# K and V of the context for the second block: tiles of their own, and another place in the order of work

## The chip, the cores and the metric

The kernel runs on one core of one Trainium2 chip. The metric is the device time of one execution in microseconds (us). The core's engines work side by side, each on its own stream of instructions: TensorE (PE; its weight loads are listed apart as PEld), VectorE (DVE), ScalarE (ACT), GpSimd (POOL) and SyncE (SP), which here mostly issues DMAs. An engine works through its own instructions in their order, and waits on semaphores for what others make.

## What is computed

Two attention blocks follow each other, all in fp32. The tokens x are 2 x 1024 rows of 256 elements, the context ctx is 2 x 64 rows of 256, and there are 16 heads of 16. Cut to what matters:

```
# block 0
q  = ln(x);  x = x + mha(q, q)                      # self attention, 1024 keys
x  = x + mha(ln(x), ln(ctx))                        # cross attention, 64 keys
h  = ln(x)                                          # 8 experts, the best 2 for each token
vals, idx = top_k(h @ router, 2);  gates = softmax(vals)
x  = x + sum_k gates_k * expert_idx_k(h)            # 256 -> 1024, gelu, -> 256

# block 1
x  = x + self_attention(ln(x))
q  = heads(ln(x) @ q_w.T)
k  = heads(ctx @ k_w.T)                             # ctx as it comes in, no norm
v  = heads(ctx @ v_w.T)
x  = x + softmax(q k^T * scale + bias) v @ ca_proj_w.T
x  = x + fc2(gelu(fc1(ln(x))))
```

The k and v of block 1 depend on nothing but ctx and two weights. They could be made at any time before block 1's first cross attention.

## The kernel before

*Stages.* The self attention of a block is a sequence of 128 cells. A cell makes scores on PE (line 796), their maxima on DVE (803), scores less the maxima on PE (807), exponentials on ACT (813) and the product with V on PE (858). Other work, cut into generators that yield estimated costs, runs between the cells. A `Stream` holds these generators as tasks; a task may begin at a cell (`first`), must be done by a cell (`last`), has marks that it waits for (`after`) and a `rank`. Behind the last cell, `stream.rest` takes the ready task of the highest rank, one step at a time, and counts time by the costs that the steps yield; a step that yields zero or less makes its task not ready for a while. All this happens while the program is built. The result is a fixed order of instructions on PE, DVE, ACT and SP; POOL's order is set by the tile framework.

*Behind the first block's cells* (from about 596 us in the profiled execution) `stream.rest` has these left: the fourth cross attention (tokens 512 to 1023 of the second sequence), which consists of two halves; `dispatch_task` for units 2 and 3 of 512 tokens (the router's logits, line 1320; ranking within the experts, lines 1373 to 1409; writing of the sorted rows, scatters on POOL); `mixture.find` and `mixture.rows`; and the first five slots. A slot is 256 rows for one expert, its weights being loaded by DMA: transposes of its rows (1610), a first layer (1644), GELU on ACT (1650), a second layer (1674), and a scatter of its result to DRAM by POOL (1689). The ranks are: cross attention up to 67, finding 65, dispatch 70, rows 75, and slot s 10-s. `norm_task` and `turned` (360) norm and transpose tokens, `project_task` (428 and 436) is an output projection and its addition to x.

*Then* `mixture.run(5, 15)` emits slots 5 to 14, in the profile from about 730 to 935 us, and block 1's cells follow, with the remaining slots at their beginning.

*The context.* `context_load` issues the DMAs for a block's two context weights (512 KB, tile `w_ctx`) and for ctx, twice 64 KB (both halves of the partitions hold a copy). `context_task` makes, in this order: for block 0 a norm; four transposes of ctx (360, called by `turned`); for block 1 a copy of them (`kvT`, 1017); K's products (1025); four evictions to `kbd` (1037), in which every second head is zeroed by a column of scales; V's products (1047); eight copies to `vbd` (1058), which fill only every second group of 16 columns, the others having been set to zero by a memset in `other_constants`. `weigh`, the weighing of a cross attention, reads `kbd` in its score products (1131) and `vbd` in its products with V (1180).

`kbd` and `vbd` are one tile each, in the pool of the constants (lines 295 and 296), 4 KB of each partition together, and serve both blocks. The second block's context is written to them only after the first block's last cross attention has read them. Its task is advanced by hand within slots 5 to 14:

```
1965        for n, _ in enumerate(mixture.run(NFULL[-1], NFIRST)):
1966            if n > 16 and n % 2 == 0:
1967                next(context, None)
```

*Memory.* Pools are opened and closed in the program. `cpool0` and `dpool0` hold the tiles of block 0's cross attentions and dispatch and are closed by `tail.close()` (line 1956). `hpool`, opened after them in the room they leave, holds block 1's head tiles, `QS` and `KS` among them; `make_heads` fills their constant rows with copies and memsets on POOL. The right side holds the slots' pools (`slotw`, `epool`).

Of the kernel before, what the change touches and what calls it, by code (L numbers as in the profile page):

```python
# [41 lines left out]
F32 = mybir.dt.float32  # L42
# [8 lines left out]
P = 128  # L51
B, S, D, H, DH = 2, 1024, 256, 16, 16
# [149 lines left out]
def two_blocks(  # L202
# [89 lines left out]

    desc = const.tile([P, E], F32, name="desc")
    bias_out = [const.tile([P, D], F32, name=f"bias_out{i}") for i in range(2)]
    kbd = const.tile([P, 2, B, 2, SK], F32, name="kbd")
    vbd = const.tile([P, B, H // 2, 32], F32, name="vbd")

    def other_constants():
        nc.gpsimd.memset(restart, 1.0)
        nc.gpsimd.memset(restart[:, :, 0:1], 0.0)  # L300
        nc.gpsimd.memset(vbd, 0.0)

    maxima = [True]

# [685 lines left out]
    def context_load(layer, pool):  # L990

        w = pool.tile([P, NCTX], F32, tag="cq", name=f"w_ctx{layer}")
        nc.sync.dma_start(out=w, in_=ctx_w[layer])
        c = pool.tile([P, B, D], F32, tag="cx", name=f"ctx{layer}")
        for u in range(2):
            nc.sync.dma_start(
                out=c[SK * u : SK * (u + 1)], in_=ctx_in.rearrange("b k d -> k b d")
            )
        return w, c

    def context_task(layer, w, c, pool):

        att = 2 * layer + 1
        kv = pool.tile([P, 2, B * P], F32, tag="p1", name=f"kvT{layer}", bufs=4)

        def src(t):
            return c[:, t, :]

        if layer == 0:
            held = yield from statistics(src, B, "kv")  # L1010
            xns = center(src, range(B), held, "kv")
            yield 0.0
            i, tp = turned(xns)
            affine(kv, i, tp, "ckv")
        else:
            i, tp = turned([src(t) for t in range(B)])
            nc.scalar.copy(kv, tp)
            free.append(i)
        yield 1.0
        yield 0.0  # L1020
        i, pk = bank()
        pk = pk[:, : 2 * B * SK].rearrange("p (g b k) -> p g b k", g=2, b=B)
        for g in range(2):
            for k in range(2):
                nc.tensor.matmul(
                    pk[:, g],
                    lhsT=w[:, X_K + k * D + g * P : X_K + k * D + (g + 1) * P],
                    rhs=kv[:, k, :].rearrange("p (b c) -> p b c", b=B)[:, :, :SK],
                    start=(k == 0),
                    stop=(k == 1),  # L1030
                )
        yield 1.0

        for u in range(2):
            for g in range(2):
                bias = C_K[att] + 2 * u + g
                nc.scalar.activation(
                    kbd[:, g, :, u, :], pk[:, g], AF.Identity, bias=cols[:, bias : bias + 1],
                    scale=cols[:, C_U + u : C_U + u + 1],
                )  # L1040
            yield 0.3
        free.append(i)
        i, pv = bank()
        pv = pv.rearrange("p (b d) -> p b d", b=B)
        for b in range(B):
            for k in range(2):
                nc.tensor.matmul(
                    pv[:, b, :],
                    lhsT=kv[:, k, b * P : (b + 1) * P],
                    rhs=w[:, X_V + k * D : X_V + (k + 1) * D],  # L1050
                    start=(k == 0),
                    stop=(k == 1),
                )
        yield 2.0
        for u in range(2):
            half = slice(SK * u, SK * (u + 1))
            for b in range(B):
                nc.scalar.copy(
                    vbd[half, b, :, DH * u : DH * (u + 1)],
                    pv[half, b, :].rearrange("p (r v d) -> p r v d", v=2, d=DH)[:, :, u, :],  # L1060
                )
        free.append(i)
        yield 0.5
# [28 lines left out]
    def weigh(layer, b, pool, w, name, held):  # L1092

        att = 2 * layer + 1
        yield -1.4
        xT = held["xT"]
        q = pool.tile([P, 2, 512], F32, tag="cq", name=f"q_{name}")
# [741 lines left out]
    def block(layer, tail, heads=None, beside=None):  # L1839

        pools = {}

        def open_pools():
            side = {"side": "right"} if layer else {}
            for p in ("cpool", "dpool"):
                pools[p] = tail.enter_context(tc.tile_pool(name=f"{p}{layer}", bufs=1, **side))

        if layer == 0:
            open_pools()
        made, ys, ready = [], [], {}  # L1850

        def arrive(n):
            if layer == 1:
                engines = (nc.gpsimd if n else nc.vector, nc.vector)
                add_results(ys[n // 2][:, n % 2], n, engines)

        def extra(stream, vpool, at_cell):
            if layer == 0:
                t = vpool.tile([P, 8, WIDE], F32, tag="v", name="fill")
                nfill = NROWS // 512  # L1860
                for n in range(nfill):
                    at_cell(n + 2, lambda n=n: fill(t, n))
                at_cell(nfill + 2, lambda: stream.made.add("filled"))
                stream.add(
                    context_task(layer, *context_load(layer, pools["cpool"]), pools["cpool"]), 9.0,
                    last=30, mark="context",
                )
            else:
                at_cell(104, lambda: made.extend(forward_weights(vpool)))
                stream.made.add("context")  # L1870
                ys.extend(
                    vpool.tile([P, 2, 2, 2, D], F32, tag="v", name=f"y{i}") for i in range(3)
                )
                for n in range(4):
                    load_results(ys[n // 2][:, n % 2], n)

                def second_batch(n0):
                    for n in range(n0, n0 + 2):
                        load_results(ys[2][:, n % 2], n)
                    for n in range(n0, n0 + 2):  # L1880
                        add_results(ys[2][:, n % 2], n, (nc.gpsimd, nc.gpsimd))
                    if n0 == 6:
                        stream.made.add("arrived")

                at_cell(0, lambda: second_batch(4))
                at_cell(3, lambda: second_batch(6))

        def when_ready(b, qh, stream, cell):
            n = 2 * b + qh
            cross_tasks(stream, layer, n, pools["cpool"], cell + 1)  # L1890
            if layer == 0:
                stream.add(
                    dispatch_task(n, pools["dpool"], lambda: stream.made.add(("counted", n))), 7.0,
                    mark=("dispatch", n),
                    after=[("cross", n), "filled"] + ([("dispatch", n - 1)] if n else [])
                    + ([("found", n)] if n > 1 else []),
                    rank=70,
                )
                if n == 1:
                    stream.add(  # L1900
                        mixture.find(2), 0.3, mark=("found", 2), after=[("counted", 1)], rank=65
                    )
                    stream.add(
                        mixture.rows(2), 0.0, mark=("rows", 2), rank=75,
                        after=[("found", 2), ("dispatch", 1)],
                    )
            elif n < 2:
                stream.add(
                    forward_norm(n, pools["dpool"], made, ready), 3.0, first=106, mark=("ready", n),
                    after=[("cross", n)],  # L1910
                )

        def around(begin):
            beside(begin)
            open_pools()

        stream, later = self_attention(layer, tail, heads, arrive, extra, when_ready, around)
        return stream, later, made, ready
# [11 lines left out]
    slotw, epool = [], []  # L1930
    mixture = Mixture(slotw, epool)
    stream, later, _, _ = block(0, tail)
    slotw.append(slots.enter_context(tc.tile_pool(name="slotw", bufs=2, side="right")))
    for n in range(2):
        epool.append(
# [13 lines left out]
    for s in range(NFULL[-1]):  # L1949
# [2 lines left out]
            mixture.slot(s), 14.4, mark=("slot", s), rank=10 - s,  # L1952
            after=[("rows", units)] + ([("slot", s - 2)] if s > 1 else []),
        )
    stream.rest(later, 64 * B + 2)
    tail.close()
    hpool = ctx.enter_context(tc.tile_pool(name="hpool", bufs=1))
    load_attention(2)
    load_attention(3)
    heads = make_heads(hpool, 1)  # L1960
    with ExitStack() as passing:

        xpool = passing.enter_context(tc.tile_pool(name="xpool", bufs=1))
        context = context_task(1, *context_load(1, xpool), xpool)
        for n, _ in enumerate(mixture.run(NFULL[-1], NFIRST)):
            if n > 16 and n % 2 == 0:
                next(context, None)
        for _ in context:
            pass

    def beside(begin):

# [164 lines left out]
```

## The time and the profile before

| what | us |
|---|---|
| median of 3 runs | 1632.26 (1632.18 to 1632.59) |
| the profiled execution | 1638.78 |
| its span, from the first to the last instruction | 1637.0 |
| PE busy in the span | 1591.4 |
| from the last cell to the slots run by themselves, 596 to 730 | 134, PE busy 121.9 |
| slots 5 to 14, 730 to 935 | 205, PE busy 205.0 |

The profile is of one execution, which took 6.5 us more than the median of the runs without a profile. Its page in forty slices, from which the stages can be read:

```profile
PE   7999999999999998999999999999999999999998
...
DVE  5796767687678647421113457876867867855400
...
PEclk9898999999999998999999999999999999999999
DMA  5234311101000105276567321000110002000000
```

Each digit is the busy share of 41 us, in tenths. Slices 1 to 14 hold block 0's cells; then come the stretch behind them, with DMA rising and DVE falling, and the slots, where DVE is nearly idle; from slice 23 on, block 1. PEclk is the clock that PE was granted, in tenths of its full speed: it is 8 in the second and fourth slice, and again in the slice from 614 to 655 us, where the fourth cross attention stands.

In views of single instructions, `banks<-kvT,w_ctx 128*128 128x128` is a tile written, the tiles read and the shapes; `x8` counts records; what stands in square brackets is how long the engine waited before it and for what.

### The profile page before, as it was taken

To read this page: it belongs to the slowest core of one execution; us is meant where nothing else is said; L and a number is where in the kernel's file an instruction comes from. 1 tells how busy PE (TensorE), PEld (TensorE's weight loads), DVE (VectorE), ACT (ScalarE), POOL (GpSimd) and SP (SyncE) were. 2 spreads that over 40 slices of the span, in tenths; PEclk is the share of its full clock that TensorE was granted. 3 is DMA by queue.
4 is the path that set the end of the run, shared out by engine and by line. 5 is a ranking of instruction groups with operands and counts; after the bars stand their busy time and mean duration, and the time that the engine had idled before them with its cause. 6 is when DMAs were issued, how large, how long until landed. Compare 5 with 4: busy or idle time off the path is not lost.

```text
span 1637.0 us, 28319 instructions
## 1 busy us (share of the span) xinstructions
PE 1591.4 (97%) x10710; PEld 882.4 (54%) x10710; DVE 982.7 (60%) x2094; ACT 912.9 (56%) x1767; POOL 410.6 (25%) x545
## 2 busy tenths in 40 slices
PE   7999999999999998999999999999999999999998
PEld 3433444544543446878888753344344435446766
DVE  5796767687678647421113457876867867855400
ACT  3486767676765753333322327876776676674321
POOL 2243423134235202141112032411321323321010
PEclk9898999999999998999999999999999999999999
DMA  5234311101000105276567321000110002000000
GB/s 157 111 132 171 131 27 34 28 21 47 14 21 34 53 30 188 78 270 216 176 204 241 91 65 33 21 27 17 38 39 19 25 14 83 15 14 21 14 13 26
DMA packets 55751, 121.07 MB, mean 74 GB/s; under 512 B 12218, under 2 KB 26428, under 8 KB 55228
## 3 DMA queue, kind: packets, MB, share of 16 engines
q1 hardware_dynamic: 51772, 109.07, 20.9%
q0 software_dynamic: 3456, 9.51, 1.6%
q8 instruction: 86, 1.41, 0.4%
q10 hardware_dynamic: 384, 0.66, 0.2%
q14 instruction: 53, 0.43, 0.1%
HBM read 71.68 MB, written 38.88 MB: 68 GB/s over the span
## 4 chain that ended last, share of the span: by engine, by line
PE 89%; DVE 7%; issue 1%; ACT 1%; DMA 1%; another core or an unknown queue 1%; POOL 0%; SPq 0%; DVEq 0%; POOLq 0%; ACTq 0%
PE banks L807 16%; PE banks L796 15%; PE banks L858 14%; PE banks L1674 8%; PE banks L1644 8%; PE banks L626 4%; PE banks L428 3%; PE banks L1816 3%; PE banks L1804 3%; DVE mx_s L803 3%; PE banks L1131 2%; PE banks L596 2%; PE banks L1167 2%; PE banks L360 2%; PE banks L1101 2%
## 5 line engine op out<-in xcount | busy, mean ns | idle before, releaser
L803 DVE TENSOR_REDUCE mx_s<-banks 128x1 f32<-128x512 f32 x1024 | 634.7, 682 | 221.2 <-PE banks L796 214.9
L813 ACT ACTIVATE pt_s<-banks 128x512 f32<-128x512 f32 x1024 | 532.6, 609 | 155.5 <-PE banks L796 124.4
L796 PE MATMUL banks<-KS,QS 16*128 16x512 f32 x2048 | 539.5, 633 | 4.0 <-ACT part_s L870 1.6
L807 PE MATMUL banks<-qb_s,KS 32*128 32x512 f32 x2048 | 519.2, 623 | 6.6 <-DVE qb_s L706 3.7
L871 POOL TENSOR_TENSOR acc_s<-acc_s,part_s 128x512 f32<-128x512 f32 x141 | 179.4, 1272 | 442.2 <-ACT part_s L870 441.5
L807 PEld LDWEIGHTS banks<-qb_s,KS 32*128 32x128 f32 x2048 | 181.3, 187 | 178.6 <-DVE mx_s L803 104.4
L858 PE MATMUL banks<-pt_s,v_s 128*20 128x512 f32 x2048 | 264.1, 607 | 1.5 <-DVE mx_s L803 1.0
L796 PEld LDWEIGHTS banks<-KS,QS 16*128 16x128 f32 x2048 | 201.1, 186 | 76.8 <-issue 37.3
L1674 PE MATMUL banks<-w_slot,h_s 128*128 128x256 f32 x640 | 145.4, 383 | 3.0 <-ACT h_s L1650 3.0
L858 PEld LDWEIGHTS banks<-pt_s,v_s 128*20 128x20 f32 x2048 | 43.2, 99 | 187.5 <-ACT pt_s L813 132.1
L1674 PEld LDWEIGHTS banks<-w_slot,h_s 128*128 128x128 f32 x640 | 121.7, 192 | 23.5 <-ACT h_s L1650 3.4
L870 ACT COPY part_s<-banks 128x512 f32<-128x512 f32 x155 | 92.7, 598 | 65.1 <-PE banks L858 54.5
L1683 DVE SCALAR_TENSOR_TENSOR ys<-banks,gate,b 128x256 f32<-128x256 f32 x40 | 19.3, 483 | 174.2 <-PE banks L1674 166.3
L1650 ACT ACTIVATE h_s<-banks,w_slot 128x256 f32<-128x256 f32 x104 | 43.7, 471 | 111.6 <-issue 65.3
L1689 POOL DMA_INDIRECT results<-ys,to x40 | 38.7, 967 | 255.0 <-DVE ys L1683 211.2
L1644 PE MATMUL banks<-xsT,w_slot 128*128 128x256 f32 x416 | 95.6, 381 | 0.7 <-ACT xsT L367 0.7
L1644 PEld LDWEIGHTS banks<-xsT,w_slot 128*128 128x128 f32 x416 | 77.4, 190 | 14.9 <-DVE mx_s L803 2.3
L1152 POOL TENSOR_TENSOR sc_c<-sc_c,mx_c 128x512 f32<-128x512 f32 x38 | 40.0, 1054 | 102.4 <-DVE mx_c L1151 102.4
L626 PE MATMUL banks<-xT_s,w_att 128*128 128x512 f32 x128 | 64.7, 642 | 0.0
L1807 ACT ACTIVATE h_f<-banks,w_ff 128x512 f32<-128x512 f32 x32 | 22.0, 687 | 73.9 <-PE banks L1804 73.9
L1650 ACT ACTIVATE h_s<-banks,spare 128x256 f32<-128x256 f32 x56 | 23.4, 471 | 62.8 <-issue 31.3
L1816 PE MATMUL banks<-w_ff,h_f 128*128 128x256 f32 x256 | 57.3, 380 | 0.0
(269 smaller groups left out, 1651.4 us busy)
## 6 DMA issues: line engine op xcount, KB each, us to landing
w_slot<-in_ff_w_dram SPq DMA_DIRECT2D x40, 576.0 KB
sorted_rows<-fill SPq DMA_DIRECT2D x36, 520.0 KB
w_slot<-in_ff_w_dram SPq DMA_DIRECT2D x26, 514.0 KB
whole<-acc_s SPq DMA_DIRECT2D x30, 256.0 KB
spare<-in_ff_w_dram SPq DMA_DIRECT2D x14, 514.0 KB
xs<-sorted_rows SPq DMA_DIRECT2D x20, 260.0 KB
y<-results SPq DMA_DIRECT2D x16, 256.0 KB
QS<-stq_s SPq DMA_DIRECT2D x124, 32.0 KB
```

The costliest lines, as they stand in the source:

```text
L626: nc.tensor.matmul(p, lhsT=w[:, at + k * D + pair * P : at + k * D + (pair + 1) * P], rhs=xT[b][:, k, blk * 512 : (blk + 1) * 512], start= ...
L796: nc.tensor.matmul(sc, lhsT=QS[h % 4][r, qc * P : (qc + 1) * P], rhs=K[r, kh * 512 : (kh + 1) * 512], start=True, stop=True,)
L803: return i, lambda: nc.vector.tensor_reduce(mx[h][:, qc, j, kh : kh + 1], sc, AX.X, ALU.max)
L807: nc.tensor.matmul(sc, lhsT=K[r, n * P : (n + 1) * P], rhs=QB[h][r, :], start=True, stop=True)
L813: nc.scalar.activation(pt, sc, AF.Exp, scale=SCALE)
L858: nc.tensor.matmul(o[32 * j : 32 * j + VW, :], lhsT=V[b][:, cell % 8, 4 * g + j, :], rhs=exps.pop((cell, j)), start=(cell == cells[0]), st ...
L870: nc.scalar.copy(part, o)
L871: helper().tensor_tensor(acc[h], acc[h], part, ALU.add)
L1644: nc.tensor.matmul(ph[:, n, :], lhsT=w[:, at : at + P], rhs=xT[:, k, :], start=(k == 0), stop=(k == 1),)
L1650: nc.scalar.activation(h1[:, f, :], ph[:, n, :], AF.Gelu, bias=w[:, W_B1 + f : W_B1 + f + 1])
L1674: nc.tensor.matmul(py, lhsT=h1[:, f, h * P : (h + 1) * P], rhs=w[:, f * D : (f + 1) * D], start=(f == 0), stop=(f == 7),)
L1816: nc.tensor.matmul(py[:, n, :], lhsT=h1[:, f, t * P : (t + 1) * P], rhs=w2[:, f * D : (f + 1) * D], start=(f == 0), stop=(f == 7),)
```

## The change

`kbd` and `vbd` become two pairs, one for each block, made by a new function `context_places`. The first block's pair stands in its `cpool0`; the second's in a new pool `kpool` on the right side, opened behind the first block's cells, with a memset of its `vbd` on POOL there. `context_task` and `weigh` pick the pair of their block.

With that the second block's context no longer has to follow the first block's last reads. Its task is now a task of the stream behind the first block's cells, of rank -20 (every other task there stands above it) and cost 6.0; `context_load` is called where the task is added, so its three DMAs are issued there. Its tiles stand in `xpool`, which is now open around `stream.rest`. `mixture.run(5, 15)` runs with nothing between.

```diff
@@ two_blocks
-    kbd = const.tile([P, 2, B, 2, SK], F32, name="kbd")
-    vbd = const.tile([P, B, H // 2, 32], F32, name="vbd")
+    kbds, vbds = {}, {}
+
+    def context_places(layer, pool):
+
+        kbds[layer] = pool.tile([P, 2, B, 2, SK], F32, name=f"kbd{layer}")
+        vbds[layer] = pool.tile([P, B, H // 2, 32], F32, name=f"vbd{layer}")
+
 
     def other_constants():
...
-        nc.gpsimd.memset(vbd, 0.0)
+        nc.gpsimd.memset(vbds[0], 0.0)
@@ context_task and weigh
         att = 2 * layer + 1
+        kbd, vbd = kbds[layer], vbds[layer]
@@ block
         if layer == 0:
             open_pools()
+            context_places(0, pools["cpool"])
@@ two_blocks, behind the cells of block 0
     stream, later, _, _ = block(0, tail)
+    kpool = ctx.enter_context(tc.tile_pool(name="kpool", bufs=1, side="right"))
+    context_places(1, kpool)
+    nc.gpsimd.memset(vbds[1], 0.0)
     slotw.append(slots.enter_context(tc.tile_pool(name="slotw", bufs=2, side="right")))
...
-    stream.rest(later, 64 * B + 2)
+    with ExitStack() as passing:
+
+        xpool = passing.enter_context(tc.tile_pool(name="xpool", bufs=1))
+        stream.add(
+            context_task(1, *context_load(1, xpool), xpool), 6.0, mark="context1", rank=-20
+        )
+        stream.rest(later, 64 * B + 2)
     tail.close()
...
-    with ExitStack() as passing:
-
-        xpool = passing.enter_context(tc.tile_pool(name="xpool", bufs=1))
-        context = context_task(1, *context_load(1, xpool), xpool)
-        for n, _ in enumerate(mixture.run(NFULL[-1], NFIRST)):
-            if n > 16 and n % 2 == 0:
-                next(context, None)
-        for _ in context:
-            pass
+    for _ in mixture.run(NFULL[-1], NFIRST):
+        pass
```

The order of instructions that results is this. On PE the four transposes of ctx follow those of slot 0's rows and precede the router's product of unit 2 (1320); K's products follow slot 0's first layer, of which one half lies behind the last ranking products of unit 2 (1381); V's products stand between the first score products (1131) and the first transposes of scores (1167) of the fourth cross attention. On DVE the second addition of the output projections moves behind the operations on the logits, and unit 2's row addresses (1386 to 1409) move ahead of the centring for the fourth cross attention. On ACT the copy `kvT`, the evictions to `kbd` and those to `vbd` move with their products. On SP the three context DMAs move from behind block 1's attention weights to right behind the second half of slot 0's weights. On POOL there is the memset more, and the filling of block 1's head tiles moves from behind the scatters of unit 3 to ahead of the result scatters of slot 1.

More of the change, by code (lines that the diff above doesn't have):

```diff
@@ L1094, in weigh @@
         att = 2 * layer + 1
+        kbd, vbd = kbds[layer], vbds[layer]
         yield -1.4
```

## The prediction

> **What bounds the kernel now.** I read the page first (busy shares and chain), then the windows around the place where the context work of the second block stands and around the place it goes to, then the timelines of those two places.
>
> ```profile
> span 1637.0 us, 28319 instructions
> PE 1591.4 (97%) x10710; PEld 882.4 (54%) x10710; DVE 982.7 (60%) x2094; ACT 912.9 (56%) x1767; POOL 410.6 (25%) x545
> ...
> PE 89%; DVE 7%; issue 1%; ACT 1%; DMA 1%; another core or an unknown queue 1%; POOL 0%; SPq 0%; DVEq 0%; POOLq 0%; ACTq 0%
> ```
>
> TensorE sets the end: busy 97% of the span, 89% of the chain. So work costs what it costs on PE, unless it is put where PE is idle. The windows say where that is (us of the window, then busy us of PE, PEld, DVE, ACT, POOL, granted clock, DMA):
>
> ```profile
> 604.99:631.50 26.51, 25.56 (x110) 18.06 (x109) 17.63 (x92) 11.16 (x19) 7.71 (x8) 1.00 0.18 51
> 631.50:635.23 3.73, 0.00 (x0) 0.00 (x1) 3.63 (x5) 0.74 (x2) 3.45 (x3) 0.86 0.93 349
> 635.23:666.00 30.77, 29.36 (x241) 23.94 (x242) 16.88 (x39) 13.18 (x23) 0.99 (x1) 0.79 0.50 173
> ...
> 730.00:935.00 205.00, 205.00 (x987) 176.39 (x990) 49.36 (x190) 68.17 (x161) 29.40 (x29) 1.00 0.59 195
> ```
>
> From 730 to 935 (the slots of experts, where the context task is woven in today) PE is never idle: whatever leaves that stretch shortens the kernel by its own length. Behind the first block's cells (604.99 to 666) PE is idle 0.95 us, then 3.73, then 1.41. The timeline of PE where the three pieces stand now, each with the instruction after it:
>
> ```profile
> 765.45 0.60 PE L360 MATMUL banks<-ident,ctx 128*128 128x128 f32 x4
> 765.89 1.89 PE L1644 MATMUL banks<-xsT,w_slot 128*128 128x256 f32 x8
> ...
> 774.96 1.05 PE L1025 MATMUL banks<-kvT,w_ctx 128*128 128x128 f32 x8
> 775.85 3.62 PE L1674 MATMUL banks<-w_slot,h_s 128*128 128x256 f32 x16
> ...
> 790.11 1.89 PE L1047 MATMUL banks<-w_ctx,kvT 128*128 128x256 f32 x8
> 791.83 3.62 PE L1674 MATMUL banks<-w_slot,h_s 128*128 128x256 f32 x16
> ```
>
> Read the starts, not the durations, since matmuls overlap. The path through the transposes is 765.89-765.45 = 0.44 us, through K's products 0.89, through V's 1.72. And the place they go to, with what PE waited for:
>
> ```profile
> 616.87 0.41 PE L1381 MATMUL banks<-before_m,ones 128*128 128x32 f32 x2 [0.30 <-DVE before_m L1373]
> ...
> 621.68 0.76 PE L360 MATMUL banks<-ident,xn_c 128*128 128x128 f32 x4 [0.64 <-DVE xn_c L348]
> ...
> 635.23 3.10 PE L1131 MATMUL banks<-kbd,q_c 32*128 32x128 f32 x32 [3.74 <-ACT q_c L1108]
> 638.91 1.12 PE L1167 MATMUL banks<-ident,sc_c 128*128 128x128 f32 x4 [0.57 <-DVE sc_c L1152]
> 640.23 1.11 PE L1167 MATMUL banks<-ident,sc_c 128*128 128x128 f32 x4 [0.21 <-DVE sc_c L1152]
> ```
>
> The small waits are for DVE (routing of unit 2, norm and maxima of the last cross attention). The wait of 3.74 is on an ACT instruction that itself stood 7.08 us behind what the chain of waits calls "another core or an unknown queue"; I come back to it.
>
> [...]
>
> ```profile
> 632.05 3.20 DVE L1509 COPY end<-ntu 128x16 f32<-128x16 f32 x1
> 632.72 2.49 POOL L420 TENSOR_TENSOR x_sb<-x_sb,bias_out 128x512 f32<-128x512 f32 x2
> ```
>
> The copy of 16 elements ends with the second POOL addition. [...] after the idle 3.73 us the clock is 0.50 until about 648, hence the mean of 0.79 above. [...]slot 0's 1.15 MB are issued at 596.46 and 596.99 and the DMA engines move them until 601.6.
>
> **The change, part by part.**
>
> *Removed from the slots (730 to 935).* Four transposes, K's eight and V's eight matmul records (each fp32 product of the program is two records): 0.44+0.89+1.72 = 3.05 us of pure PE path. ACT's nine evictions (one of 0.59, four of 0.46, four of 0.26) leave too; ACT is busy 68 of 205 us there, worth nothing. SP loses three issues (w_ctx, two of ctx, 1.8 us from 729.00) ahead of the next rows at 731.43; PE waits for no transfer after that, worth nothing. Gain 3.05.
>
> *Transposes, now ahead of the router's product (L1320).* At 604.99, after slot 0's transposes: +0.44. ctx must have landed. The three DMAs now stand on SP right behind slot 0's weights, before the register load that waits for the next table (about 627), so they issue by about 599 while SP and the DMA engines are idle. Behind 601.6 come 0.63 MB at the some 0.29 MB per us of the slot's weights: landed near 603.8 (an estimate from these numbers). 1.2 us to spare: no wait. Bound: 0 to +1.5.
>
> *K's products, behind the second part of slot 0's first layer:* +0.89. They and the 0.44 precede the last q projection, where PE was idle 0.30 and 0.64. But the change also reorders DVE: the first output projection moves behind the router's logits (they come 1.94-0.44 = 1.5 us earlier), the second addition to x waits for a projection ending about 611.5 instead of 610.6, and unit 2's row addresses (0.65 us) go ahead of the centring. Added up on DVE, the centred tiles come at about 622.4 instead of 621.9; PE arrives then at about 622.1. Some 0.3 us of idle time stay at each place. Net: 1.33 minus 0.94 plus 0.6 = +1.0 at the q projection. Bound: 0 (all absorbed) to +1.33.
>
> *V's products, between the first score products (L1131) and the first transposes of scores (L1167):* 1.72. Here PE waits for DVE, which takes 1.33 us for each tile of maxima and subtraction (mx_c at 637.44, 638.77, 640.10). At full clock sixteen records of L1131 take about 1.16 us (648.79 to 649.94), so the first scores are written in 2.3, and the second subtracted tile comes about 3.9 us after the start: 1.2 us of idle beyond the first transposes, 0.7 more at the fourth tile. V fits; what spills is caught at the fourth tile. Cost 0, bound +1.7 if PE is at half clock there (1.72 becomes 3.44, cover 0.78 plus the fourth tile).
>
> *ACT evictions.* kvT 0.59 ahead of the logits' bias: ACT is idle 2.72 before that. Four of K, 1.6 us, after slot 0's GELU and before the second norm's affine: ACT has an idle 2.87 there. Four of V, 0.85, behind the exponentials: idle 2.00. Nothing.
>
> *POOL.* A memset (0.5 us) behind the last cell, where POOL then idles until 621.59: nothing. And a move that the diff doesn't show: with 4 KB taken out of the constants and put into the context pool, the second block's keys no longer overlie the routing pool, and their fill (five copies, four memsets, 707.81 to 714.7, 6.9 us) stands before slot 1's result scatters, waiting for the last cross attention's end (about 666). Behind it on POOL waits the scatter of 673.67: 666+6.9 = 672.9, in time. [...] while DVE wants b (671.61) and xd_m (673.31): up to 1.4 us late, PE needs xd_m at 676.16, they end at 674.73. Cost 0, bound +1.
>
> *Sum:* -3.05+1.0 = -2.05 (bounds -3.05 to about +2). The profiled execution took 1638.78 (span 1637.0); the runs' median is 1632.26, 6.5 less. I read the unexplained waits (3.74 here, another 2.96 at 702.70) as mostly particular to the profiled execution and put the sum on the median: **1630.2**. About 0.2%, 3.3 us, is what a measurement of this kernel can tell from no change; this is below it.
>
> **Rivals.**
>
> *The half clock goes away.* If the 3.7 us wait is there in ordinary runs too, PE arrives 1 us later at it[...] Against: the 6.5 us between profile and median say that the wait mostly isn't there. Price: L1131's 32 and 16 records 3.10 and 2.08 instead of 2.3 and 1.16, L1167 1.97 instead of 1.09, L1180 with L1190 3.6 (645.18 to 648.79) instead of 1.9: 4.3 us, half of it behind DVE, so about -2 more, and the +1.0 is absorbed: 1632.26-3.05-2 = 1627.2.
>
> [...] The bound of +1 above falls due: 1631.2, same verdict as mine.
>
> *ctx lands late (the slower side).* PE works in order, so the transposes hold the router, both projections and slot 0 behind them; each us past 604.99 is a us[...] Against: no other transfer is queued. For: from 730 to 740, with other weights queued, the DMA engines are full [...]. [...]
>
> **Numbers.** Mine [...] 0.45 (1629.0 to 1632.5), half clock gone or some other wait shortened 0.41, ctx late or another new wait 0.14. Faster by over 0.2% 0.41, within 0.45, slower 0.14. Range 1626.0 to 1633.8: it leaves out the late ctx and a few hundredths at the fast end.
>
> **What would show it.** Right: no L1025, L1047 or ctx between 730 and 935; ctx's transposes at about 605 with no wait on a DMA; V's products followed by L1167 with a smaller wait on sc_c; the step from the last cell to the slots about 1 us longer, the slots 3.05 shorter. Wrong: a bracket with ctx<-in_ctx_dram at the transposes; the KS fill with DVE rows of over 1 us beside it and PE waiting for xd_m; a clock row at 1.00 through 635 to 650.

## The result, and the profile after

| | runs | median, us | lowest to highest |
|---|---|---|---|
| before | 20 | 1635.86 | 1629.99 to 1641.99 |
| after | 20 | 1628.80 | 1620.45 to 1634.37 |

The ratio is 0.9957 (95% interval 0.9945 to 0.9970): 7.0 us faster, 4.9 to 9.0. The forecast was a time of 1630.2 and a gain of 2.05. The time came within 1.4 us by luck: the three runs shown beforehand were low ones (1632.3, where 20 runs have 1635.9), and the gain is more than three times what was forecast, so two errors nearly cancel. The ratio, not the time, is what has to be explained.

The windows of the changed kernel, cut at four starts on PE: the transposes of slot 0's rows (598.18), the last q projection (622.37), the first scores of the last cross attention (628.82), the transposes of slot 1's rows (644.34); then a stretch of slots, cut at the same two instructions in both kernels. Columns: us of the window, busy us of PE, PEld, DVE, ACT and POOL, granted clock, DMA share, GB/s.

```profile
598.18:622.37 24.19, 23.76 (x121) 18.87 (x120) 17.00 (x87) 13.71 (x26) 5.53 (x6) 1.00 0.08 29
622.37:628.82 6.45, 3.59 (x9) 1.33 (x7) 2.17 (x2) 0.74 (x2) 5.51 (x6) 1.00 0.96 290
628.82:644.34 15.52, 14.88 (x152) 12.24 (x153) 13.92 (x30) 6.98 (x14) 1.13 (x2) 0.89 0.90 329
...
720.52:919.03 198.51, 198.51 (x949) 170.87 (x947) 47.38 (x181) 64.81 (x149) 28.14 (x29) 1.00 0.57 191
```

The same windows of the kernel before:

```profile
604.39:627.90 23.51, 22.57 (x109) 17.33 (x108) 16.77 (x87) 11.59 (x20) 4.84 (x5) 1.00 0.07 24
627.90:635.23 7.33, 3.59 (x9) 1.33 (x8) 4.82 (x9) 0.74 (x2) 6.33 (x6) 0.93 0.89 286
635.23:653.33 18.10, 16.68 (x144) 13.27 (x145) 12.69 (x23) 6.47 (x10) 0.99 (x1) 0.65 0.79 279
731.33:932.90 201.57, 201.57 (x970) 173.67 (x968) 46.42 (x181) 67.41 (x158) 28.58 (x29) 1.00 0.59 192
```

Last row: 201.57-198.51 = 3.06 us less, all of it PE work, as forecast. First row: 0.68 more. But the second row is 0.88 shorter, and the third is 2.58 shorter although V's products were put into it: its clock is 0.89 instead of 0.65. These two rows are what the sum on record had no term for. The timeline of PE shows how:

```profile
598.62 0.60 PE L365 MATMUL banks<-ident,ctx 128*128 128x128 f32 x4
...
612.88 1.05 PE L1031 MATMUL banks<-kvT,w_ctx 128*128 128x128 f32 x8
...
622.37 3.60 PE L1108 MATMUL banks<-xT_c,w_att 128*128 128x512 f32 x8
628.82 1.72 PE L1138 MATMUL banks<-kbd,q_c 32*128 32x128 f32 x32 [2.86 <-ACT q_c L1115]
630.48 3.66 PE L1053 MATMUL banks<-w_ctx,kvT 128*128 128x256 f32 x8
633.93 1.09 PE L1174 MATMUL banks<-ident,sc_c 128*128 128x128 f32 x8
```

The transposes of ctx wait for nothing. The wait for q_c is 2.86 instead of 3.74. V's products (3.66 at half clock) stand where PE waited for maxima, and from 634 on PE runs at full clock; in the kernel before it ran at half clock until 648. (Line numbers are higher by 5 to 7 in the changed kernel: 1138 is 1131 of before, 1174 is 1167, 1108 is 1101, 1115 is 1108.)

The two profiled executions differ by 13.8 us, of which 6.2 lie ahead of 605 us, where nothing was changed; half clock in block 0's cells comes and goes between executions (10.2 us of it at 139 us in the one, 3.4 in the other). So I compare starts within the stretch, and times only as ratios.

### The profile page after: what moved, and what is told of

It reads as the page before. It is cut to its first block, busy times and chain, and to the rows that moved or that the text cites. A ratio compares the mean times of both kernels' runs of the same rounds, so it can differ in the third digit from the quotient of the medians.

```text
span 1623.2 us, 28319 instructions
## 1 busy us (share of the span) xinstructions
PE 1579.5 (97%) x10710; PEld 876.8 (54%) x10710; DVE 985.1 (61%) x2094; ACT 912.9 (56%) x1767; POOL 411.0 (25%) x546
## 4 chain that ended last, share of the span: by engine, by line
PE 89%; DVE 7%; ACT 1%; issue 1%; DMA 1%; another core or an unknown queue 1%; POOL 0%; SPq 0%; DVEq 0%; POOLq 0%; ACTq 0%
PE banks L812 16%; PE banks L801 14%; PE banks L863 13%; PE banks L1651 8%; PE banks L1681 8%; PE banks L631 4%; PE banks L433 3%; PE banks L1823 3%; PE banks L1811 3%; DVE mx_s L808 3%; PE banks L1138 2%; PE banks L601 2%; PE banks L1174 2%; PE banks L1108 2%; PE banks L365 2%; PE banks L709 1%
```

## The experiments

Twelve runs, on four chips (again, mem, noctx and warm on one; after2, v_early and late_w on another; after3, noctx2, again2 and both on a third; noscat on a fourth); each ratio is to the kernel before on the same chip. Every row has one profile, so a single difference of 1 or 2 us in it can be chance. The table has the same cuts in every profile: from slot 0's transposes to the q projection, to the scores, to slot 1's transposes; how long PE's clock was half around this third part; and from slot 0's transposes to the first cell products of block 1. All in us, worked out as differences of starts.

| kernel, label | to q | q to scores | scores to slot 1 | half clock | to block 1 | ratio (95%) |
|---|---|---|---|---|---|---|
| before, first profile | 23.51 | 7.33 | 18.10 | 13.7 | 360.7 | |
| before, again2 | 23.49 | 7.34 | 17.81 | 13.7 | 360.3 | 0.9997 (0.9981 to 1.0012) |
| changed, first profile | 24.19 | 6.45 | 15.52 | 3.4 | 353.2 | 0.9957 (0.9945 to 0.9970) |
| changed, after2 | 24.17 | 6.60 | 16.61 | 6.8 | 354.6 | 0.9965 (0.9943 to 0.9986) |
| changed, after3 | 24.17 | 6.62 | 15.51 | 3.4 | 356.6 | 0.9962 (0.9949 to 0.9975) |
| noctx2 | 23.74 | 6.54 | 17.81 | 10.2 | 356.8 | 0.9954 (0.9939 to 0.9970) |
| v_early | 24.18 | 6.59 | 18.11 | 10.2 | 357.6 | 0.9979 (0.9967 to 0.9991) |
| late_w | 23.49 | 4.45 | 17.84 | 6.8 | 357.4 | 0.9977 (0.9965 to 0.9989) |
| both | 24.16 | 6.60 | 15.51 | 3.4 | 356.2 | 0.9960 (0.9947 to 0.9973) |
| before, again (chip without the wait) | 23.50 | 3.53 | 15.19 | 3.4 | 349.2 | 0.9997 (0.9981 to 1.0013) |
| mem (same chip) | 23.50 | 3.53 | 14.54 | 0 | 348.5 | 1.0001 (0.9987 to 1.0016) |
| noctx (same chip) | 23.75 | 3.52 | 14.51 | 0 | 345.9 | 0.9983 (0.9971 to 0.9994) |
| warm (same chip) | 23.50 | 5.25 | 16.84 | 6.8 | 352.4 | 1.0008 (0.9994 to 1.0021) |
| noscat | 24.00 | 3.52 | 14.51 | 0 | 345.9 | 0.9883 (0.9853 to 0.9913) |

### again: is the wait for q_c always there?

The kernel before, with nothing changed.

> The kernel before, unchanged. Both theories: ratio 1.000, time of each run between 1629 and 1642. In the profile, from the transposes of slot 0's rows to those of slot 1's: 48.9 us if the half clock after the wait for the last q_c belongs to this kernel; about 46.3 if the half clock in the first profile was chance (then the change's gain beyond the 3.06 us of the slots is chance too). The wait for q_c: 3.5 to 3.8 us in any case.

On this chip the kernel before takes 1620.86 us (59 runs), 15 us less than in the first comparison, and its profile has no wait for q_c at all. Its timeline of PE:

```profile
621.54 3.60 PE L1101 MATMUL banks<-xT_c,w_att 128*128 128x512 f32 x8
625.07 1.72 PE L1131 MATMUL banks<-kbd,q_c 32*128 32x128 f32 x32
627.83 0.66 PE L1167 MATMUL banks<-ident,sc_c 128*128 128x128 f32 x4 [1.04 <-DVE sc_c L1152]
```

The scores follow the projection without a bracket. "3.5 to 3.8 us in any case" was wrong, and so was the time, 1629 to 1642. The wait is there on some chips and not on this one; whether it goes with the chip or with the occasion no run separates, since each chip was used on one occasion. The next three runs were on this chip too.

### mem: the memory part alone

The changed kernel's tiles, pools and memset, with the old loop over slots 5 to 14:

```diff
-        stream.add(
-            context_task(1, *context_load(1, xpool), xpool), 6.0, mark="context1", rank=-20
-        )
...
+        context = context_task(1, *context_load(1, xpool), xpool)
+        for n, _ in enumerate(mixture.run(NFULL[-1], NFIRST)):
+            if n > 16 and n % 2 == 0:
+                next(context, None)
```

> The memory part alone: two pairs of kbd and vbd, kpool, the memset more and the earlier KS and QS fill on POOL; the context task stays in slots 5 to 14. Theory A (the gain is the 3.06 us out of the slots plus the wait for q_c filled): same as before, within 1 us, all marks as before. Rival M (part of the gain comes from the memory, through the fill on POOL): 2 to 4 us faster than before, and the stretch from 660 to 730 us shorter.

No difference (1.0001; 2.1 us faster to 2.6 slower). On every engine but POOL its instructions stand in the same order as before; on POOL the memset is added and the fill of KS and QS moves. So the gain has to come from moving the context's work (on a chip with the wait this run was not made). The moved fill can be seen in the changed kernel, on POOL and beside it on DVE:

```profile
660.00 1.03 POOL L514 COPY KS<-cols 128x1024 f32<-128x1024 f32 x1
660.98 0.52 POOL L516 MEMSET QS<- 128x512 f32 x1
661.44 1.03 POOL L514 COPY KS<-cols 128x1024 f32<-128x1024 f32 x1
```

```profile
660.14 1.38 DVE L323 TENSOR_SCALAR rs_m<-root_m 128x4 int32<-128x4 int32 x1
661.55 0.94 DVE L327 TENSOR_TENSOR root_m<-rs_m 128x4 f32<-128x4 f32 x1
662.53 0.16 DVE L328 TENSOR_TENSOR root_m<-root_m,root_m 128x4 f32<-128x4 f32 x1
```

Operations on 128x4 elements, of which the last takes 0.16 us, take 1.38 and 0.94 here, and both end with an operation of POOL (at 661.5 and 662.5), as the copy of 16 elements did that took 3.20 at 632.05 in the kernel before. What holds them no run shows. PE's transposes of xd_m at 667.17 have no wait, so it costs nothing.

### noctx: the moved work taken out, on the chip without the wait

The changed kernel without the block 1 context's transposes, products and evictions; kbd is set to zero instead. All else is in its place.

```diff
-            i, tp = turned([src(t) for t in range(B)])
-            nc.scalar.copy(kv, tp)
+            i, _ = bank()
             free.append(i)
...
-        for g in range(2):
+        for g in range(2) if layer == 0 else ():
...
-        for b in range(B):
+        for b in range(B) if layer == 0 else ():
```

> The change with the second block's context left out: no transposes of ctx, no K and V products and none of their evictions (kbd is set to zero by a memset), every other instruction in its place. Theory A (the wait for q_c ends when the DMA traffic lets it, so what stands ahead of it fills it, and the shorter wait spares the half clock): not faster than the changed kernel, 0 to 3 us slower, the wait for q_c 3.4 to 3.9 us instead of 2.86, half clock behind it, 48.5 us or more from slot 0's transposes to slot 1's (46.16 with the work). Rival B (the moved work costs what my sum said, 1 us on the path): 1 us faster than the changed kernel, 45 us between these marks.

2.8 us faster than before (1.0 to 4.7), which agrees with the 3.06 us of work that left the slots. There was no wait for the work to fill, with it or without it, so this run doesn't tell theory A from rival B. It does show one term of the sum: 23.75 us to the q projection instead of 23.50, with no product added. The 0.25 can't be the moved work, which is absent; what is left of the change there is the order of the other work.

### warm: useless products put into the wait

The kernel before, with two products whose result nobody reads, between the last q projection and the scores:

```diff
+        if name == "c03":
+            i, p = bank()
+            for _ in range(2):
+                nc.tensor.matmul(
+                    p, lhsT=w[:, X_Q : X_Q + P], rhs=xT[:, 0, :], start=True, stop=True
+                )
+            free.append(i)
```

> The kernel before with two products more (128x512, 1.8 us by the rows of the q projection, their result never read) between the last q projection and the first score products, inside the wait for q_c. Theory A: faster than before by 2 to 4 us, the wait shrinks from 3.74 to about 1.9 us, no half clock behind it, 46 us between the transposes of slots 0 and 1 instead of 48.94. Rival B (the wait moves with PE, or the clock has nothing to do with it): same or up to 1.8 us slower.

This chip has no wait, so the run can't say whether a filled wait pays. It says what filling costs where there is none:

```profile
627.13 1.88 PE L1116 MATMUL banks<-xT_c,w_att 128*128 128x512 f32 x4
628.94 1.72 PE L1138 MATMUL banks<-kbd,q_c 32*128 32x128 f32 x32
```

From q to scores it takes 5.25 instead of 3.53, so the whole 1.72 is on the path. Behind the scores 1.65 more is lost, with 6.8 us of half clock there instead of 3.4. The timed runs show less of it: 1.3 us slower (1.0 faster to 3.4 slower).

### after2, after3, again2: the change where the wait is

> The changed kernel, unchanged. In the four runs before this one the wait for the last q_c was not there at all (3.53 us from the q projection to the scores instead of 7.34). Theory A2 (the change is worth 3.06 us in the slots less what the moved work costs behind the cells, and the rest of the 7.0 us was the wait for q_c, which comes and goes with the session): where the wait is absent, 1.5 to 2.5 us faster than before, 24.2 us from slot 0's transposes to the q projection, about 27.7 to the scores, 42.5 to 43.5 to slot 1's transposes; where it is there, some 7 us faster and 46 us to slot 1's transposes. Rival (the 7 us are the change's own, whatever the session): ratio 0.9957 here too.

> The changed kernel once more, beside three others on the same chip. Theory A2: if the kernel before has the wait for the last q_c on this chip, 5 to 7 us faster than before, q projection to scores 6.4 to 6.7 us; if it hasn't, 1.5 to 2.5 us faster, 3.5 us between these and 42.5 to 43.5 us from slot 0's transposes to slot 1's. Rival (the gain is the change's own): 5 to 7 us faster either way.

> The kernel before, for its profile on this chip. Theory A2: q projection to scores either 3.5 us (no wait) or about 7.3 us with 10 to 14 us of half clock behind it, and then 48 to 49 us from slot 0's transposes to slot 1's, as in the first profile. Rival (the half clock of the first profile was chance): 45 to 46.5 us there with the wait.

Both chips have the wait: 1637.4 and 1638.5 us before. The change gives 5.7 us (2.3 to 9.3) and 6.2 us (4.1 to 8.4). again2 has the wait to 0.01 us as in the first profile, and the same 13.7 us of half clock; the half clock behind q_c was no chance of one execution. Nor does it need a slow one: the profiled execution of again2 took 1630.9 us, less than the 1632.3 that the prediction started from. Over the profiles with the wait, from slot 0's transposes to slot 1's, the mean is 48.8 us before (two) and 46.6 after (three): 2.2 us. With the 3.06 of the slots that makes 5.2, inside all three intervals. Up to block 1 the means are 360.5 and 354.8, 5.7 us apart.

The mean granted clock of all timed runs says the same without any choice of a profile. On the chip of after2 it is 0.9794 before (46 runs) and 0.9823 after (9); on that of after3, 0.9787 (19) and 0.9816 (5). The time lost to the clock is (1 - clock) times the span: 33.7 and 28.8 us on the first, 34.9 and 30.0 on the second, 4.9 less on each. PE's work is the same in both kernels and only stands elsewhere, so the gain must be less half clock and less waiting; by these means the clock is the larger part of it (an estimate, which counts half clock during a wait as lost too).

### noctx2: the moved work taken out, where the wait is

> The change with the second block's context left out (no transposes, K, V, nor their evictions), as before. Without the wait for q_c it was 2.8 us faster than before, which is the work taken out. Theory A2: where the wait is there, the time is the changed kernel's or up to 2 us more, since the work fills the wait and the wait is longer without it (3.4 to 3.7 us instead of 3.0), with as much half clock behind it as in the kernel before; where it is absent, 0.5 to 1.5 us faster than the changed kernel. Rival B (the moved work costs its length on the path): 1 to 3 us faster than the changed kernel either way.

In the profile most of the stretch behaves as theory A2 says. The timeline of PE:

```profile
632.73 1.72 PE L1137 MATMUL banks<-kbd,q_c 32*128 32x128 f32 x32 [2.95 <-ACT q_c L1114]
636.25 1.12 PE L1173 MATMUL banks<-ident,sc_c 128*128 128x128 f32 x4 [1.80 <-DVE sc_c L1158]
637.66 1.09 PE L1173 MATMUL banks<-ident,sc_c 128*128 128x128 f32 x4 [0.29 <-DVE sc_c L1158]
```

and the window behind:

```profile
632.73:650.54 17.81, 15.08 (x144) 11.88 (x145) 13.89 (x30) 6.47 (x10) 1.01 (x2) 0.71 0.78 284
```

PE has 2.09 us of further waits behind the scores where the changed kernel has V's products, the clock is half for 10.2 us, and slot 1's transposes come 48.09 us after slot 0's. With three pieces of work more the changed kernel needs 46.30 on the same chip. The wait for q_c is not longer than with the work (2.95), against what I had expected of A2: the work does not shorten that wait. What differs is the cover behind the scores. The mean clock of the runs leans the same way, 0.9793 (6 runs) beside 0.9787 before and 0.9816 for the changed kernel, but single runs of noctx2 spread from 0.976 to 0.983.

The times don't settle it. 0.9954 and 0.9962 have overlapping intervals, and taken alone they lean to rival B, by 1.3 us. What the profiles show for the stretch, the few timed runs (6 and 5) neither confirm nor exclude for the whole.

### v_early: V's products into the wait for q_c

```diff
             free.append(i)
             yield 1.72
+        if name == "c03":
+            for c in between:
+                if c == 2.0:
+                    break
...
-            context_task(1, *context_load(1, xpool), xpool), 6.0, mark="context1", rank=-20
+        between = context_task(1, *context_load(1, xpool), xpool)
+        stream.add(between, 6.0, mark="context1", rank=-20)
```

> The changed kernel with V's products of the context placed between the last q projection and the first score products, ahead of the place where PE may wait for q_c, instead of behind the first score products. Theory A2: where the wait is absent, the same as the changed kernel or up to 1.7 us slower (the cover behind the scores is lost); where it is there, 1 to 2 us faster than the changed kernel, and the wait under 1.2 us. Rival (V's products are not hidden behind the scores): the same as the changed kernel in both cases.

```profile
631.90 1.89 PE L1053 MATMUL banks<-w_ctx,kvT 128*128 128x256 f32 x8
635.06 1.72 PE L1142 MATMUL banks<-kbd,q_c 32*128 32x128 f32 x32 [1.27 <-ACT q_c L1115]
638.57 1.12 PE L1178 MATMUL banks<-ident,sc_c 128*128 128x128 f32 x4 [1.79 <-DVE sc_c L1163]
```

V's products cost nothing in the wait: the scores come at the same place (30.77 us behind slot 0's transposes, as in after2), and the wait shrinks to 1.27. But the waits for the maxima are open again (1.79 and 0.30), 10.2 us of half clock follow, and 18.11 us pass to slot 1 instead of 16.61. The gain is 3.4 us (1.5 to 5.4), not above the changed kernel's 5.7 (2.3 to 9.3) beside it. Theory A2 expected 1 to 2 us more. So the part of the theory that laid the gain on the wait for q_c falls; in the profiles what counts is that PE has work while DVE makes the maxima.

Why, can be read from the clock in the profiles with the wait. In the first profile of before it changes at 600.07, 603.48, 634.20, 647.86, 705.88 and 709.30, which are 1, 9, 4, 17 and 1 times 3.413 us apart; all 18 changes of that profile, and all 16 of the first one of after, stand a whole number of this length apart. So I cut the time into windows of 3.41 us, from the start of the half clock backward and forward. For each profile: how far into its window the first scores start, PE's busy time in the last window at full clock, and in each of the half windows behind it, all in us.

| profile | V's products | scores start at | last full window | half windows |
|---|---|---|---|---|
| before | in the slots | 1.03 | 0.70 | 2.39, 2.63, 3.41, 3.42 |
| again2 | in the slots | 1.62 | 1.29 | 1.80, 2.63, 3.41, 3.42 |
| noctx2 | none | 1.51 | 1.72 | 1.51, 3.41, 3.41 |
| v_early | ahead of the scores | 0.89 | 1.72 | 2.13, 3.41, 3.41 |
| after | behind the scores | 1.60 | 1.81 | 3.41 |
| after2 | behind the scores | 0.91 | 1.32 | 2.50, 3.42 |
| after3 | behind the scores | 1.24 | 2.18 | 3.41 |
| both | behind the scores | 1.19 | 2.23 | 3.41 |

V's products don't prevent the half clock. Behind the scores they fill the windows in which it is half, and it ends after one or two; without them PE still waits for maxima there (1.80 and 0.29 us in noctx2), and it lasts three or four. Where the scores fall in a window doesn't separate the two groups: both have early and late starts. late_w, below, has no V there and two half windows, 3.34 and 3.41 full, behind a much shorter wait.

### late_w and both: what makes the wait?

Slot 1's weights issued behind the sorted rows (late_w on the kernel before, both on the changed one):

```diff
-            self.load(1)
+            if last:
+                self.load(1)
```

> The kernel before with slot 1's weights (four DMAs, 1.1 MB) issued on SP behind the three loads of sorted rows instead of ahead of them, so that they don't run beside the scatters of the sorted rows. Theory W (the wait for q_c is made by these loads and the scatters in the DMA engines at the same time): where the wait is there in the kernel before, it goes away, and 5 to 9 us with it; where it is absent, within 1 us of before. Rival (it is made by something else): the wait stays as it is in the kernel before.

> The changed kernel with slot 1's weights issued behind the loads of the sorted rows on SP. Theory A2 with W: where the wait is there, faster than the changed kernel by 0 to 3 us (some of the wait that the context's work filled is gone, so the gains of the two don't add up), q projection to scores about 4.4 us; where it is absent, as the changed kernel within 1 us. Rival (two gains of 3.8 and 5.7 us that add up): 9 us faster than before where the wait is there.

In late_w the wait was 0.85 us and 3.8 us (1.8 to 5.7) were gained. That is in the direction of theory W, though W had the wait gone and 5 to 9 us. In both the wait was 3.01, as without the edit, and the gain that of the changed kernel (6.6, 4.4 to 8.7). The views of both: SP's DMAs, ACT, and POOL.

```profile
634.98 2.00 SPq L1565 DMA_DIRECT2D xs<-sorted_rows  x3
637.48 3.21 SPq L1581 DMA_DIRECT2D w_slot<-in_ff_w_dram  x4
```

```profile
635.77 1.26 ACT L1115 ACTIVATE q_c<-banks,cols 128x512 f32<-128x512 f32 x2 [6.19 <-remote]
```

```profile
629.22 0.96 POOL L1424 DMA_INDIRECT sorted_rows<-xd_m,at_m  x1 [0.30 <-issue]
630.49 0.96 POOL L1424 DMA_INDIRECT sorted_rows<-xd_m,at_m  x1 [0.30 <-issue]
631.75 0.96 POOL L1424 DMA_INDIRECT sorted_rows<-xd_m,at_m  x1 [0.30 <-issue]
```

SP issued nothing before 634.98, and ACT still waited 6.19 us for "remote" while the scatters ran back to back on POOL. q_c began 5.86 us behind the start of the projection (629.91); in noscat, below, it takes 1.92. The loads are not needed for the wait, so W falls as its cause. Why late_w had less of it stays open: it is the kernel before with the edit, and ran on another chip than both.

### noscat: the scatters taken out

The changed kernel without the sixteen scatters of the sorted rows of units 2 and 3; result rows that are then not written are zeroed beforehand.

```diff
         for t in range(4):
-            for k in range(2):
+            for k in range(2) if unit < 2 else ():
```

> The changed kernel without the sixteen scatters of sorted rows of units 2 and 3 (the rows keep their fill, and the result rows that are then never written are set to zero by eight DMAs during block 0's cells); everything else in its place. The run with the weights issued late showed the wait for q_c at 3.01 us with nothing but scatters moving in the DMA engines. Theory S (the scatters hold back the semaphores that q_c waits for, and the half clock follows from that wait): q projection to scores 3.5 us on any chip, 27.7 us from slot 0's transposes to the scores and 42.0 to 43.5 to slot 1's, and the wait for h_s in front of 704 us gone too; this is also what the moved work costs without the wait, to be set beside 41.6 to 42.2 of the kernel before on the chip without it. Time 9 to 14 us under the kernel before where that has the wait, 2 to 4 us where it hasn't. Rival (the wait is made by something else): 6.4 to 6.7 us from q projection to scores where the kernel before has 7.3.

```profile
623.31:626.84 3.53, 3.53 (x9) 1.33 (x8) 2.93 (x16) 0.69 (x1) 1.20 (x2) 1.00 0.44 105
626.84:641.34 14.50, 13.55 (x153) 10.82 (x153) 12.06 (x19) 7.36 (x14) 0.00 (x0) 1.00 1.03 398
```

```profile
625.23 0.69 ACT L1115 ACTIVATE q_c<-banks,cols 128x512 f32<-128x512 f32 x1 [2.43 <-PE banks L1108]
```

The kernel before took 1638.5 us on this chip, as on those with the wait (neither kernel was profiled there). Here q_c follows its products (2.43, for PE), no window is half, and the wait for h_s in front of 704 us is gone as well (21.2 us between the two groups of slot transposes that stand at 700.37 and 726.44 in the first profile of before, where it is 26.1; 24.2 in that of after; 21.2 on the chip without the wait). The time is 19.2 us under the kernel before (14.3 to 24.1), more than the 9 to 14 expected; where the rest comes from was not traced. Weight loads ran beside (0.44 and 1.03 of the DMA engines) and held up nothing, so it is the scatters that make the wait, by this one profile. The order of the other work being that of the changed kernel, this profile stands in for the changed kernel without the wait, which was not run itself: 42.03 us to slot 1, 345.9 to block 1, beside 41.57 and 348.5 of mem. By that estimate, across two chips, the change is worth 2.6 us without the wait: 3.06 less 0.46.

## Why the prediction was right and where it was not

- *The slots, -3.05:* 3.06. Right.
- *The transposes of ctx and their DMAs:* no wait. Right; the rival with the late ctx is out. (Its ground: from 730 to 740 the DMA share of the kernel before was 1.04. How long a load took there was not shown.)
- *K and the transposes, +1.0 at the q projection:* +0.68 with the wait, +0.50 in noscat, of which 0.25 came without any moved work (noctx). The mechanism was right, the size somewhat large.
- *V's products, 0:* in noscat and noctx 14.51 us pass from the scores to slot 1, with and without V's products. Right where there is no wait: V is hidden behind DVE's maxima.
- *POOL's fill, 0:* mem, 1.0001. Right; the rival in which its bound of +1 falls due, counted with mine in the 0.45, is out. That DVE would be up to 1.4 us late beside it was the author's estimate; two operations took 1.38 and 0.94 there. *ACT and SP, 0:* no run moved these alone, but from 598 to 644 PE's only waits in the changed kernel are 0.29 for before_m, 2.86 for q_c and 0.64 for sc_c, none for a moved eviction or a transfer.
- *The sum, -2.05:* without the wait -2.6 (the estimate above). The working was right for that condition.
- *The step that failed:* "I read the unexplained waits (3.74 here, another 2.96 at 702.70) as mostly particular to the profiled execution and put the sum on the median". The wait for q_c was 3.74 again in again2, and the kernel before took 1636 to 1638 on all chips of the comparisons but one; the 6.5 us between profile and median lie within the spread of single runs (1630.0 to 1642.0), and again2's profiled execution was a short one with the same wait. So the half clock behind it was in ordinary runs too, and the rival "the half clock goes away", with K's cost absorbed (the scores come 30.8 us behind slot 0's transposes before, 30.6 to 30.8 after, and 30.3 without the work in noctx2), is nearest to what happened: it said -5.05, the marks say -5.2, the timed runs -7.0, -5.7 and -6.2. Its number was better than its argument. It took the half clock to be gone once PE arrives 1 us later at the wait, which no trace had shown. But the wait of 2.86 still has 3.4 us of half clock behind it, and v_early shows that a still shorter wait, 1.27, leaves 10.2. What shortens the half clock here is V's products behind the scores (3.4 to 6.8 us, against 10.2 in noctx2 and v_early), which I had priced at zero but not at a gain.

What remains between 5.2 and 7.0 is inside the intervals. The gain of over 0.2%, to which I had given 0.41, is what the runs show.

## What to carry over

Here a stage in which TensorE waits again and again for another engine was paid twice, in the waits and in the clock: in noctx2 2.09 us of waits behind the scores and 10.2 us of half clock, in after3, with V's products there, no such wait and 3.4 us. Work moved there was better than free, and it paid beside the waits that recur, not in the longest one. A wait whose releaser the profile can't name is no artefact until a second profile lacks it; ask for the spread of single runs before taking the gap between a profile and a median for the profile's own cost. And a gain that hangs on such a wait depends on where the kernel runs: 5 to 7 us where the wait was, and an estimated 2.6 where it wasn't.

## What the runs showed of the hardware

- Scatters of 128 rows each, issued back to back by POOL every 1.27 us, held up the start of q_c by some 3.9 us (both against noscat) with no load beside them; on the chip of again the same scatters, also every 1.27 us, held up nothing (q_c 1.92 us behind the projection's start). With them gone the changed kernel takes 4.6 us less from slot 0's to slot 1's transposes and 4.1 less around the wait for h_s (42.0 and 21.2 against the means of its three profiles, 46.6 and 25.3). That is more than this change brought. Spacing the scatters out, or replacing them, was not tried.
- Half clock came in 3.4, 6.8, 10.2 or 13.7 us, multiples of the 3.41 us by which its changes stand apart. In the first profile of before it began at 634.20, while PE was still waiting (631.50 to 635.23), and ended at 647.86. How busy PE was in one window did not settle the clock of the next: in v_early the 3.4 us ahead of the half clock at 637.6 had 1.7 us of waits and otherwise score products of 32 rows, and in v_early and noctx2 a window of 3.41 us busy was followed by another at half clock, in after by full clock. Behind the wait of 3.74 us PE was busy 2.39 to 3.42 us in each of four half windows. What in the work decides it was not tried.
